# Two chained pair-mixing layers on one core: x before the weights at the start, a full-height bias product, and the first 16 rows of x rebuilt in stage 2 instead of transposed in stage 3

## The chip, the cores and the metric

The kernel runs on one core of a Trainium2 chip. The time is the device time of one execution in microseconds (us). The engines that matter are TensorE (PE, with its weight loads PEld), VectorE (DVE), ScalarE (ACT), GpSimd (POOL) and SyncE (SP), whose work here is to issue DMAs. Each engine executes its own instructions in program order and waits for the others by semaphores. DMAs are issued from SP's, ACT's and POOL's queues.

## What is computed

The input x has 384 x 384 positions (i, j) with 128 channels, all in f32. Two layers follow each other. Of the reference, what matters is this (its names shortened):

```python
z = _layernorm(x, norm_g, norm_b)
left = (z @ Wl + bl) * jax.nn.sigmoid(z @ Wlg + blg)
right = (z @ Wr + br) * jax.nn.sigmoid(z @ Wrg + brg)
core = jnp.einsum('bikh,bjkh->bijh', left, right)
zo = _layernorm(core, onorm_g, onorm_b) @ Wout + bout
g = jax.nn.sigmoid(x @ Wg + bg)
x1 = x + g * zo
...
left = x1 @ W_left + b_left + (x1 @ W_eq + b_eq)
right_sum = jnp.sum(x1 @ W_right + b_right, axis=2, keepdims=True)
out = left * right_sum * jax.nn.sigmoid(x1 @ W_gate + b_gate)
y = _layer_norm(out @ W_out + b_out + x1, ln_scale, ln_bias)
```

The first layer needs a sum over k for every channel h (einsum), so nothing of `core` is complete before all of x has been projected. The second layer works on one row i at a time.

## The kernel before, in words

It runs in three stages. Everything that passes through `seq` keeps its program order on its engine, so the order of the work is the order in which the Python code issues it.

**Opening and stage 1 (lines 99 to 399).** 144 chunks of eight rows and 128 positions k are loaded by SP (`load_chunk`, line 112). The first chunk is loaded in two halves, and SP goes on with the other half and three more chunks, while ACT's queue loads the four projection matrices with two columns of the first norm (`stage`, line 130) and the bias row (line 131). A "step" is four rows. DVE takes mean and variance of each row (`stats`), POOL makes the reciprocal root and the shift (`powers`, `shift`), PE transposes the shifted rows (line 271, in the first step line 288), ACT copies them out of PSUM (`zt`), PE multiplies each with the 128 x 512 matrix `wz` (line 323), ACT applies the sigmoid (line 332), DVE the product (line 334). The shifted transposed rows go to DRAM as `xt_d` (line 294), the shifts as `nd_d` (line 302), the products as `lr_d`.

Before the first such product, `wz` must be made. `busy` (line 147) runs two filler products of 128 x 512 on PE; `fold` (line 154) then makes, for each half of the columns, one product with `m1` (line 163, it needs the weights and two POOL instructions, lines 159 and 160) and one with the bias row `brow`, which has one partition (line 164). `weights` (line 168) adds the two on DVE.

**Stage 2 (lines 443 to 528).** For each channel h, SP loads left and right (`load_h`, lines 93 and 94; called for h+3 in line 506), POOL copies the right part to its own tile (`fill`, lines 468 to 475), PE makes nine products of 128 x 384 (line 493), ACT copies the result (line 502) and squares it, DVE adds to the two sums that the second norm needs, and SP stores to `core_d` (line 509). There are three buffers for loaded channels and two for `rr`. In the last channel DVE and ACT make the reciprocal root of the first 128 rows (lines 419 to 441), which is stored to `rstd_d` (line 525) and loaded back in broadcast (`rt`, line 590).

**Stage 3 (lines 534 to 858).** One turn t of the loop in line 789 does, in this order: `front`, DMA issues, `scale_core(t)`, `layer0(t - 2)`, `gated_left(t - 3)` and, from turn 11 on, `layer1` and the rest of the second layer. `front(f)` runs ahead: it transposes row f of x (three PE transposes into one bank, line 632) if f is below TR = 16, with a copy on ACT or DVE (lines 634 and 636), or takes the row from the tile `xts`, which SP loaded with `nd_d` in broadcast (line 568) and to which POOL's queue added `xt_d` by an accumulating DMA (line 576, from turn 9 on). It also makes the gate of row f - 4 (line 621, sigmoid in line 623). `scale_core` multiplies `core` with the reciprocal root: in the first four rows through a PE broadcast product (`pb`, line 654) and DVE, later with `rt` on POOL (line 657). `layer0` makes `x1T` from it (lines 666 to 669). PSUM is divided in four banks of the pool `ps2` (tag `py`) and four of `ps` (tag `bank`), each used in turn.

Of the kernel before, what the change touches and what calls it, by code (L numbers as in the profile page):

```python
# [8 lines left out]
F32 = mybir.dt.float32  # L9
AF = mybir.ActivationFunctionType  # L10
# [9 lines left out]
def triangle_then_gated_row_kernel(ctx: ExitStack, tc: tile.TileContext, a: dict, out: bass.AP):  # L20
# [10 lines left out]


    nc = tc.nc
    x = a["x"].rearrange("b i j c -> (b i) j c")
# [9 lines left out]
    RG = 4  # L44
    A = 9
    L = 4
    TR = 16
# [6 lines left out]
    xt_d = dpool.tile([C, N, NB, P], F32, name="xt_d")  # L54
    nd_d = dpool.tile([N, N], F32, name="nd_d")

    def seq(ins):

        return tc.keep_in_program_order(ins)
# [4 lines left out]
    def load(dst, src, queue=nc.sync):  # L64
        seq(queue.dma_start(out=dst, in_=src))
# [15 lines left out]
    with ExitStack() as ctx2:  # L81
# [17 lines left out]
        with tc.tile_pool(name="p1w", bufs=6, side="right") as wp, \  # L99
# [28 lines left out]
            wst, g0, b0 = stage[:, 0:4 * H], stage[:, 4 * H:4 * H + 1], stage[:, 4 * H + 1:4 * H + 2]  # L128
            brow, m1, d = stage[0:1, 5 * H:9 * H], stage[:, 9 * H:10 * H], stage[:, 10 * H:10 * H + 1]
            load(stage[:, 0:4 * H + 2], a["L0_side_W"], nc.scalar)  # L130
            load(brow, a["L0_side_b"].rearrange("(o h) -> o h", o=1), nc.scalar)
            load_chunk(0, slice(4, XR))
# [13 lines left out]

            def busy(n):

                for _ in range(n):
                    seq(nc.tensor.matmul(  # L150
                        p0, lhsT=avg, rhs=avg.unsqueeze(1).to_broadcast([P, 4, P]), start=True, stop=True
                    ))

            def fold():

                busy(2)
                seq(nc.gpsimd.tensor_tensor(d, b0, g0, ALU.subtract))
                seq(nc.gpsimd.tensor_tensor(m1, avg, d.to_broadcast([P, P]), ALU.mult))  # L160

                for p, gs in zip((p0, p1), halves):
                    seq(nc.tensor.matmul(p[:, gs], lhsT=m1, rhs=wst[:, gs], start=True, stop=False))
                    seq(nc.tensor.matmul(p[:, gs], lhsT=avg[0:1, :], rhs=brow[:, gs], start=False, stop=True))

# [277 lines left out]
        with tc.tile_pool(name="p2r", bufs=2, side="right", reuse_waits="tile") as rrp, \  # L443
# [14 lines left out]
            def fill(h):  # L458

                if h < H:  # L460
# [15 lines left out]
                    if h == 0:  # L476
                        stay()

            fill(0)
# [54 lines left out]
    with ExitStack() as ctx3:  # L534
# [13 lines left out]

        def work_x(name):

            return lp.tile([P, N], F32, tag="x", name=name)

# [5 lines left out]
        def load_x(i0):  # L558

            if i0 < TR:  # L560
                xt = xin[i0] = xp.tile([P, RG, N], F32, tag="xt", name="xn")
                seq(nc.sync.dma_start(
                    out=xt.rearrange("p i (b c) -> p i b c", b=NB),
                    in_=x[i0:i0 + RG].rearrange("i (b p) c -> p i b c", p=P),
                ))
            elif i0 < N:
                xt = xts[i0] = xp.tile([P, RG, N], F32, tag="xt", name="xt")
                seq(nc.sync.dma_start(
                    out=xt.rearrange("p i j -> p (i j)"),
                    in_=nd_d[i0:i0 + RG].rearrange("i j -> (i j)").partition_broadcast(P),  # L570
                ))
# [8 lines left out]

        def load_core(i0):
            if i0 < N:
                ct = inp.tile([P, RG, N], F32, tag="ct", name="ct")

                for hs in (slice(0, H),) if i0 > 0 else (slice(0, H - 16), slice(H - 16, H)):
                    seq(nc.sync.dma_start(out=ct[hs], in_=core_d[i0:i0 + RG, hs].rearrange("i h j -> h i j")))
                rt = None
# [28 lines left out]
        def front(f):  # L616

            r = rows.get(f - L)
            if r:
                pg = bank("pg")  # L620
                seq(nc.tensor.matmul(pg[:, :N], lhsT=wg0, rhs=r["xT"], start=True, stop=True))  # L621
                gT = r["gT"] = work("gT", fp)
                seq(nc.scalar.activation(gT, pg[:, :N], AF.Sigmoid, bias=bg0))  # L623
            if f < N:
                i0, n = f // RG * RG, f % RG
                if f >= TR:
                    xT = xts[i0][:, n]
                else:
                    xT = work_x("xT")
                    pxt = ps2.tile([P, 512], F32, tag="py", name="pxt") if f < A else bank("pxt")  # L630
                    for s in cols:
                        seq(nc.tensor.transpose(pxt[:, s], xin[i0][:, n, s], ident))
                    if 4 <= f < A:
                        seq(nc.vector.tensor_copy(xT, pxt[:, :N]))
                    else:
                        seq(nc.scalar.copy(xT, pxt[:, :N]))
                rows[f] = {"xT": xT}

# [20 lines left out]
        def layer0(i):  # L659

            r = rows[i]
            m, n = group[i]
            if n == 0:
                quad[m] = {"tot": sp.tile([P, 16], F32, tag="tot", name="tot")}
            pr = bank("pr")
            seq(nc.tensor.matmul(pr[:, :N], lhsT=wc, rhs=r["cs"], start=True, stop=True))  # L666
            seq(nc.vector.scalar_tensor_tensor(pr[:, :N], pr[:, :N], bz, r["gT"], ALU.add, ALU.mult))
            x1T = r["x1T"] = work_x("x1T")
# [223 lines left out]
```

## Time and profile before

| | us |
|---|---|
| three runs, median | 3288.17 |
| lowest and highest | 3287.86, 3288.30 |
| the profiled execution, its own time | 3288.61 |
| its span, from the first to the last record | 3286.8 |

| stretch of the span | us | PE busy | DMA, mean busy share | moved, GB/s |
|---|---|---|---|---|
| 0 to 11.11: until the first product of stage 1 | 11.11 | 9.49 | 0.83 | 213 |
| 11.11 to 1130.80: stage 1 | 1119.69 | 1119.43 | 0.89 | 257 |
| 1130.80 to 1873.90: stage 2 | 743.10 | 743.04 | 0.91 | 282 |
| 1873.90 to 1928.10: first turns of stage 3 | 54.20 | 53.16 | 0.94 | 306 |
| 1928.10 to 3272.90: the rest of stage 3 | 1344.80 | 1341.16 | 0.95 | 265 |
| 3272.90 to 3286.80: after the last product | 13.90 | 0.00 | 0.38 | 108 |

The table is the view of busy time by stretch. "PE busy" counts the modelled ends of the products, which overlap their successors; the time from one product's start to the next is the better measure of what PE gives, and the prediction uses that. An f32 product appears as two records, a transpose as one.

### The profile page before, as it was taken

The numbers are of one execution on the slowest core, as the hardware profiler recorded it, in microseconds if no ns is written. First come the engines' busy times: TensorE is split into PE (matmuls) and PEld (weight loads), VectorE is DVE, ScalarE is ACT, GpSimd is POOL, SyncE is SP. The second block draws the span as 40 slices with busy tenths as digits, with TensorE's granted clock in tenths as the row PEclk, the third lists the DMA queues.
The fourth block names the chain that finished last, engine by engine and source line by source line (L and its number), as shares of the span: only waits on it lengthen the run. The fifth ranks groups of instructions, "written<-read, shape, count | busy, mean of one in ns | idle before, by whom it ended". The sixth has DMA issues, their size and how long they took to land.

```text
span 3286.8 us, 48304 instructions
## 1 busy us (share of the span) xinstructions
PE 3266.3 (99%) x12458; PEld 1987.4 (60%) x12458; DVE 2491.7 (76%) x8019; ACT 1936.1 (59%) x4056; POOL 2289.6 (70%) x3299
## 2 busy tenths in 40 slices
PE   9999999999999999999999999999999999999998
PEld 4444444444444566666666666667777777777776
DVE  7777777777777655555555588888888888888888
ACT  4555555555555533333333467677777777777776
POOL 5555555555555466665656578888888888888997
PEclk9999999999999999999999999999999999999999
DMA  6998998999999499999998999999999999999994
GB/s 165 275 280 257 277 281 258 276 280 264 273 279 269 147 280 287 281 282 286 281 282 284 285 294 264 279 281 270 271 280 275 272 273 280 271 272 273 266 254 127
DMA packets 921492, 873.70 MB, mean 266 GB/s; under 512 B 24657, under 2 KB 836177, under 8 KB 921218
## 3 DMA queue, kind: packets, MB, share of 16 engines
q1 hardware_dynamic: 906528, 796.03, 78.2%
q0 software_dynamic: 13312, 72.55, 12.8%
q8 instruction: 102, 1.67, 0.2%
q10 hardware_dynamic: 1378, 2.04, 0.2%
q14 instruction: 172, 1.41, 0.1%
HBM read 508.63 MB, written 361.89 MB: 265 GB/s over the span
## 4 chain that ended last, share of the span: by engine, by line
PE 96%; POOL 2%; ACT 1%; DVE 1%; issue 1%; DMA 0%; POOLq 0%; ACTq 0%; DVEq 0%
PE pr L323 30%; PE pc L493 22%; PE py L695 7%; PE pr L666 7%; PE pl L684 7%; PE pg L621 7%; PE pg L683 7%; PE pt L271 4%; PE py L696 4%; POOL cs L657 1%; POOL rs L715 1%; POOL yt L765 1%; ACT py L730 0%; DMA core_d<-ct 0%; PE pq L643 0%
## 5 line engine op out<-in xcount | busy, mean ns | idle before, releaser
L323 PE MATMUL pr<-wz,zt 128*128 128x512 f32 x2304 | 1040.0, 593 | 0.0
L332 ACT ACTIVATE sg<-pr,rs 128x256 f32<-128x256 f32 x1152 | 483.8, 471 | 496.6 <-PE pr L323 363.3
L493 PE MATMUL pc<-rr,lrh 128*128 128x384 f32 x2304 | 743.3, 486 | 0.3 <-DVE lr L334 0.3
L334 DVE SCALAR_TENSOR_TENSOR lr<-pr,rs,sg 128x256 f32<-128x256 f32 x1152 | 504.7, 480 | 267.4 <-ACT sg L332 218.2
L323 PEld LDWEIGHTS pr<-wz,zt 128*128 128x128 f32 x2304 | 414.2, 190 | 411.0 <-issue 345.9
L493 PEld LDWEIGHTS pc<-rr,lrh 128*128 128x128 f32 x2304 | 452.0, 196 | 291.8 <-issue 1.1
L730 ACT ACTIVATE py<-py,nm,rs 128x128 f32<-128x128 f32 x1149 | 494.4, 431 | 200.2 <-POOL rs L719 122.1
L657 POOL TENSOR_TENSOR cs<-ct,rt 128x384 f32<-128x384 f32 x380 | 427.9, 1130 | 11.2 <-PE pr L666 6.6
L695 PEld LDWEIGHTS py<-wo,u 128*128 128x128 f32 x2304 | 376.6, 191 | 97.5
L504 DVE TENSOR_TENSOR csum<-csum,ct 128x1152 f32<-128x1152 f32 x127 | 179.3, 1412 | 333.5 <-ACT ct L502 333.5
L765 POOL TENSOR_TENSOR yt<-yt,lnb 128x384 f32<-128x384 f32 x380 | 426.0, 1122 | 3.1 <-DVE yt L759 3.1
L502 ACT COPY ct<-pc 128x1152 f32<-128x1152 f32 x127 | 142.2, 1120 | 445.2 <-PE pc L493 436.0
L695 PE MATMUL py<-wo,u 128*128 128x128 f32 x2304 | 402.1, 275 | 0.0
L252 POOL TENSOR_SCALAR sd<-mv 128x8 f32<-128x8 f32 (+1 forms) x145 | 28.7, 198 | 425.2 <-DVE mv L239 425.0
L262 POOL TENSOR_TENSOR z<-xt,nd 128x512 f32<-128x512 f32 x287 | 299.3, 1043 | 34.6 <-POOL z L262 29.4
L710 DVE BATCH_NORM_STATS2 st<-py 128x6 f32<-128x128 f32 x1152 | 265.5, 286 | 66.9 <-PE py L696 65.1
L696 PE MATMUL py<-ident,x1T 128*128 128x128 f32 x1152 | 314.0, 273 | 0.0
L666 PE MATMUL pr<-cs,wc 128*128 128x384 f32 x768 | 313.9, 490 | 0.1
L684 PE MATMUL pl<-x1T,mat_L_conv_W_left 128*128 128x384 f32 x768 | 311.0, 487 | 1.0 <-ACT gT L623 0.9
L683 PE MATMUL pg<-x1T,mat_L_conv_W_gate 128*128 128x384 f32 x768 | 310.8, 486 | 1.1 <-ACT g L686 0.9
L621 PE MATMUL pg<-xt,mat_L_conv_Wg 128*128 128x384 f32 x736 | 298.6, 487 | 1.4 <-ACT gT L623 1.4
L237 DVE BATCH_NORM_STATS2 st<-xt 128x6 f32<-128x128 f32 x1152 | 273.7, 279 | 3.9 <-DMA xt<-in_x_dram 3.9
(127 smaller groups left out, 4819.0 us busy)
## 6 DMA issues: line engine op xcount, KB each, us to landing
lr_d<-lr SPq DMA_DIRECT2D x128, 1024.0 KB, 7.1
lrh<-lr_d SPq DMA_DIRECT2D x128, 768.0 KB, 7.7
xt_d<-zt SPq DMA_DIRECT2D x288, 256.0 KB, 5.4
xt<-in_x_dram SPq DMA_DIRECT2D x143, 512.0 KB, 6.6
ct<-core_d SPq DMA_DIRECT2D x95, 768.0 KB, 6.1
rt<-rstd_d SPq DMA_DIRECT2D x95, 768.0 KB, 7.7
out_dram<-yt SPq DMA_DIRECT2D x94, 768.0 KB, 8.7
core_d<-ct SPq DMA_DIRECT2D x125, 576.0 KB, 8.8
```

The lines of the kernel that those rows point to most:

```text
L323: seq(nc.tensor.matmul(pr[:, r, :], lhsT=zts[n, q][:, 2 * half + r, :], rhs=wz, start=True, stop=True))
L332: seq(nc.scalar.activation(sg[r], pr[:, r, 2 * H:], AF.Sigmoid, scale=rs[r]))
L334: seq(nc.vector.scalar_tensor_tensor(t[:, :, c * XR + r0 + r, :], pr[:, r, :2 * H].rearrange("k (h s) -> k h s", s=2), rs[r], sg[r].rearra ...
L493: seq(nc.tensor.matmul(banks[ib], lhsT=t[:, kb, ib * P:(ib + 1) * P, 0], rhs=rr[:, kb], start=(kb == 0), stop=(kb == NB - 1),))
L621: seq(nc.tensor.matmul(pg[:, :N], lhsT=wg0, rhs=r["xT"], start=True, stop=True))
L657: seq(nc.gpsimd.tensor_tensor(cs, ct[:, i % RG], rt[:, i % RG], ALU.mult))
L666: seq(nc.tensor.matmul(pr[:, :N], lhsT=wc, rhs=r["cs"], start=True, stop=True))
L683: seq(nc.tensor.matmul(pg2[:, :N], lhsT=wgate, rhs=r["x1T"], start=True, stop=True))
L684: seq(nc.tensor.matmul(pl[:, :N], lhsT=wleft, rhs=r["x1T"], start=True, stop=True))
L695: seq(nc.tensor.matmul(py[:, s], lhsT=r["u"][:, s], rhs=r["wo"], start=True, stop=False))
L730: seq(nc.scalar.activation(py[:, s], py[:, s], AF.Identity, bias=bias, scale=scale))
L765: seq(engine.tensor_tensor(yt, yt, lnbb, ALU.add))
```

## The change

It has three parts.

**At the start**, SP issues the load of the weights itself, second, right after the first half of the first chunk; before, ACT's queue issued it. The bias row gets the full height of 128 partitions: DVE clears `brow`, the bias is loaded in its first partition, and both operands of the bias product have 128 partitions. The filler gets one more product, of 128 x 128.

**In stage 2**, a new function `early_x` puts the first 16 rows of x together: SP loads the row's shifts in broadcast (`xe`, at h = 6 + 5i), POOL's queue adds the row of `xt_d` (h = 8 + 5i), SP stores the sum in a new DRAM tensor `xf_d` (h = 11 + 5i). The tile `xe` uses the three buffers that the reciprocal roots get after stage 2.

**In stage 3**, the first 16 rows come from `xf_d` like the later ones; the transposes and their copies are gone. The gates are made in `front` for the row itself; eight rows are taken ahead before turn 0, with banks of both pools in turn, and the lead shrinks to one row. The orders of the loads of x, of `core_d` and of the roots on SP's queue change; later loads of x are issued some turns later (t + 18 in place of f + 16).

```diff
-    A = 9
-    L = 4
+    A = 8
...
+    xf_d = dpool.tile([C, TR, N], F32, name="xf_d")
...
-            brow, m1, d = stage[0:1, 5 * H:9 * H], stage[:, 9 * H:10 * H], stage[:, 10 * H:10 * H + 1]
-            load(stage[:, 0:4 * H + 2], a["L0_side_W"], nc.scalar)
-            load(brow, a["L0_side_b"].rearrange("(o h) -> o h", o=1), nc.scalar)
+            brow, m1, d = stage[:, 5 * H:9 * H], stage[:, 9 * H:10 * H], stage[:, 10 * H:10 * H + 1]
+            load(stage[:, 0:4 * H + 2], a["L0_side_W"])
...
+            seq(nc.vector.memset(brow, 0.0))
+            load(brow[0:1], a["L0_side_b"].rearrange("(o h) -> o h", o=1), nc.scalar)
...
                 busy(2)
+                busy(1, 1)
...
-                    seq(nc.tensor.matmul(p[:, gs], lhsT=avg[0:1, :], rhs=brow[:, gs], start=False, stop=True))
+                    seq(nc.tensor.matmul(p[:, gs], lhsT=avg, rhs=brow[:, gs], start=False, stop=True))
...
+            def early_x(h):
+                for n, step in enumerate((6, 8, 11)):
+                    i, odd = divmod(h - step, 5)
+                    if not odd and 0 <= i < TR:
+                        if n == 0:
+                            early[i] = rp.tile([P, N], F32, tag="ve", name="xe", bufs=NB)
+                            seq(nc.sync.dma_start(out=early[i], in_=nd_d[i].partition_broadcast(P)))
+                        elif n == 1:
+                            seq(nc.gpsimd.dma_start(
+                                out=early[i], in_=xt_d[:, i].rearrange("c b k -> c (b k)"), accum_op=ALU.add
+                            ))
+                        else:
+                            seq(nc.sync.dma_start(out=xf_d[:, i], in_=early.pop(i)))
...
             for h in range(H):
                 fill(h + 1)
+                early_x(h)
...
-        xp, lp, fp, inp = pool("p3x", 6), pool("p3l", 20), pool("p3f", A), pool("p3in", 3)
+        xp, lp, fp, inp = pool("p3x", 6), pool("p3l", 19), pool("p3f", A + 3), pool("p3in", 3)
...
+                    in_=xf_d[:, i0:i0 + RG].rearrange("c i j -> c (i j)") if i0 < TR
+                    else nd_d[i0:i0 + RG].rearrange("i j -> (i j)").partition_broadcast(P),
...
         def front(f):
+            r = rows[f] = {"xT": xts[f // RG * RG][:, f % RG]}
+            pg = ps2.tile([P, 512], F32, tag="py", name="pg") if f < A and f % 2 == 0 else bank("pg")
+            seq(nc.tensor.matmul(pg[:, :N], lhsT=wg0, rhs=r["xT"], start=True, stop=True))
+            gT = r["gT"] = work("gT", fp)
+            seq(nc.scalar.activation(gT, pg[:, :N], AF.Sigmoid, bias=bg0))
...
-        for i0 in range(0, 3 * RG, RG):
-            load_x(i0)
-        load_core(0)
-        load_x(3 * RG)
-        load_core(RG)
+        load_x(0)
+        load_x(RG)
+        load_core(0, between=lambda: load_x(2 * RG))
+        load_core(RG)
+        load_x(3 * RG)
...
-            while f < min(N + L, t + max(L, A - t // 3)):
+            while f < min(N, t + max(1, A - t // 2)):
...
-            if t >= 2 and fetched <= f + 16:
+            if t >= 2 and fetched <= t + 18:
```

`between` is called in `load_core(0)` after the load of the first 112 channels of `core_d`, so the third load of x stands between the two parts of the first load of `core_d`.

More of the change, by code (lines that the diff above doesn't have):

```diff
@@ L145, in triangle_then_gated_row_kernel, with busy @@
             p0, p1 = (pps.tile([P, 2, 4 * H], F32, tag="pr", name=n)[:, 0] for n in ("p0", "p1"))
-            def busy(n):
+            def busy(n, cols=4):
                 for _ in range(n):
                     seq(nc.tensor.matmul(
-                        p0, lhsT=avg, rhs=avg.unsqueeze(1).to_broadcast([P, 4, P]), start=True, stop=True
+                        p0[:, :cols * P], lhsT=avg, rhs=avg.unsqueeze(1).to_broadcast([P, cols, P]),
+                        start=True, stop=True,
                     ))
@@ L477, in fill @@
                         stay()
+            def early_x(h):
[11 more added lines that the diff above has]
+                            seq(nc.sync.dma_start(out=xf_d[:, i], in_=early.pop(i)))
+            early = {}
             fill(0)
@@ L547, in work @@
             return pool.tile([P, N], F32, tag=name, name=name)
-        def work_x(name):
-            return lp.tile([P, N], F32, tag="x", name=name)
         cols = [slice(b * P, (b + 1) * P) for b in range(NB)]
@@ L558, in load_x @@
         def load_x(i0):
[L560 to L566, printed above, removed]
+            if i0 < N:
                 xt = xts[i0] = xp.tile([P, RG, N], F32, tag="xt", name="xt")
@@ L569, in load_x @@
                     out=xt.rearrange("p i j -> p (i j)"),
-                    in_=nd_d[i0:i0 + RG].rearrange("i j -> (i j)").partition_broadcast(P),
+                    in_=xf_d[:, i0:i0 + RG].rearrange("c i j -> c (i j)") if i0 < TR
+                    else nd_d[i0:i0 + RG].rearrange("i j -> (i j)").partition_broadcast(P),
                 ))
@@ L579, in add_x, with load_core @@
                 ))
-        def load_core(i0):
+        def load_core(i0, between=None):
             if i0 < N:
@@ L586, in load_core @@
                     seq(nc.sync.dma_start(out=ct[hs], in_=core_d[i0:i0 + RG, hs].rearrange("i h j -> h i j")))
+                    if between and hs.start == 0:
+                        between()
                 rt = None
@@ L616, in front @@
         def front(f):
[L618 to L637, printed above, removed]
+            r = rows[f] = {"xT": xts[f // RG * RG][:, f % RG]}
[3 more added lines that the diff above has]
+            seq(nc.scalar.activation(gT, pg[:, :N], AF.Sigmoid, bias=bg0))
         def right_sums(i0, i1):
@@ L667, in layer0 @@
             seq(nc.vector.scalar_tensor_tensor(pr[:, :N], pr[:, :N], bz, r["gT"], ALU.add, ALU.mult))
-            x1T = r["x1T"] = work_x("x1T")
+            x1T = r["x1T"] = work("x1T", lp)
             seq(nc.vector.scalar_tensor_tensor(
```

## The prediction

> **What bounds the kernel now.** I read the page first: busy shares and the chain that ended last.
>
> ```profile
> PE 3266.3 (99%) x12458; PEld 1987.4 (60%) x12458; DVE 2491.7 (76%) x8019; ACT 1936.1 (59%) x4056; POOL 2289.6 (70%) x3299
> ...
> PE 96%; POOL 2%; ACT 1%; DVE 1%; issue 1%; DMA 0%; POOLq 0%; ACTq 0%; DVEq 0%
> ```
>
> TensorE is the bound in every stage, so only PE work taken away, or a wait of PE taken away, counts. All of it must come from three places: the opening, the crossing from stage 2 to 3, and stage 2 as a possible loser. So I went on to PE's timeline at both places. First the opening, weight loads (start, duration, line), then what DVE and POOL waited for:
>
> ```profile
> 5.36 0.50 PEld L163 LDWEIGHTS p<-stage 128*128 128x128 f32 x2 [2.11 <-POOL stage L160]
> 6.51 0.50 PEld L164 LDWEIGHTS p<-stage,avg 1*128 1x128 f32 x2 [0.65 <-issue]
> 9.96 0.71 PEld L288 LDWEIGHTS pt<-ident,z 128*128 128x128 f32 x4 [0.65 <-POOL sd L252]
> 12.13 0.33 PEld L323 LDWEIGHTS pr<-wz,zt 128*128 128x128 f32 x1 [0.52 <-issue]
> 12.98 0.33 PEld L323 LDWEIGHTS pr<-wz,zt 128*128 128x128 f32 x1 [0.52 <-issue]
> 13.62 0.19 PEld L323 LDWEIGHTS pr<-wz,zt 128*128 128x128 f32 x1 [0.30 <-issue]
> 14.05 0.19 PEld L323 LDWEIGHTS pr<-wz,zt 128*128 128x128 f32 x1 [0.24 <-issue]
> ...
> 4.63 0.19 POOL L159 TENSOR_TENSOR stage<-stage 128x1 f32<-128x1 f32 x1 [3.33 <-DMA stage<-in_L_side_W_dram]
> 4.95 0.49 DVE L237 BATCH_NORM_STATS2 st<-xt 128x6 f32<-128x128 f32 x2 [3.93 <-DMA xt<-in_x_dram]
> ```
>
> A pass of 512 columns takes 0.85 us (12.13 to 12.98) and from 13.62 on 0.43: PE runs at half clock until about 13.4. Weights land at 4.6, x at 4.95.
>
> The crossing, PE's products (two records per f32 product, three per transposed row):
>
> ```profile
> 1873.98 0.49 PE L632 MATMUL pxt<-ident,xn 128*128 128x128 f32 x3
> 1875.03 1.20 PE L632 MATMUL pxt<-ident,xn 128*128 128x128 f32 x9 [0.56 <-ACT ct L517]
> 1876.28 0.91 PE L621 MATMUL pg<-xT,mat_L_conv_Wg 128*128 128x384 f32 x2
> 1877.03 0.49 PE L632 MATMUL pxt<-ident,xn 128*128 128x128 f32 x3
> 1877.36 0.81 PE L621 MATMUL pg<-xT,mat_L_conv_Wg 128*128 128x384 f32 x2
> ...
> 1880.71 0.88 PE L621 MATMUL pg<-xT,mat_L_conv_Wg 128*128 128x384 f32 x2 [0.26 <-DVE xT L634]
> ...
> 1881.76 0.81 PE L654 MATMUL pb<-r,ident 128*128 128x384 f32 x2
> ```
>
> From start to start a transposed row costs 0.33 (1877.03 to 1877.36) and a 384-column product 0.645 (1888.66 to 1889.31 and on). Last, stage 2 in one step:
>
> ```profile
> 1404.01 0.36 SPq L93 DMA_DIRECT2D lrh<-lr_d  x1
> 1406.24 0.99 POOL L474 COPY rr<-lrh 128x768 f32<-128x768 f32 x1 [1.56 <-DMA lrh<-lr_d]
> 1407.17 1.54 POOL L475 COPY rr<-lrh 128x256 f32<-128x256 f32 x1
> 1409.78 1.12 ACT L502 COPY ct<-pc 128x1152 f32<-128x1152 f32 x1 [3.49 <-PE pc L493]
> ```
>
> PE's step ends about 1409.6; the copies that the next needs end at 1408.71, so a loaded channel arrives with some 0.9 us to spare.
>
> **Stage 3, what goes.** Of 16 rows 16 x 0.33 = 5.3 us of PE leave, with the 11 ACT copies (0.47 each) and 5 DVE copies (0.50) beside them. Waits leave too. I count PE from 1873.98 to the product `pr` of row 4 (line 666) at 1895.13: 21.15 us. In it are 23 products of 0.645 (9 gates, 4 `pb`, 4 `pr`, 6 of `gated_left`), 14.84, and 13 transposed rows, 4.29. So 2.0 us were waits: bank, first copies, DVE copy, first `x1T`.
>
> **Stage 3, what comes.** After: until the same product PE has 25 products (11 gates), 16.1 us, and no transpose. Waits, one by one: gate 1 wants a bank of the last channel, free when ACT's copy of line 517 ends (1874.98): 1875.03 instead of 1874.63, 0.40. Gates 1 to 7 end at 1879.55. The first `pb` wants the root; its DVE chain ends at 1880.10 now and nothing moves it: 0.65. The first `cs` on DVE wants the last 16 channels of `core_d`, issued at 1877.65 when their store has landed, 4.9 us to landing, so 1882.55; `cs` 0.56 makes `pr` of row 0 ready about 1883.2 against 1882.75: 0 to 0.45. Row 4 wants `rt`, issued at 1886.65 after the root's store, POOL at 1890.9 and 1.0 long: 1891.9 against 1891.6: 0 to 0.35. Together 1.05 to 1.85, I take 1.45. Gain: (5.3 + 2.0) - 1.45 = 5.85 us, bounds 5.4 and 6.25. ACT has its table (1.28, from 1875.75) and 8 sigmoids of 0.51 done by 1881.2; each bank is free before its product comes. The tail does not change: after 3272.9 PE is idle in both.
>
> SP's queue there: the four loads of x are as large as before, in longer rows. The fourth now stands behind `rt`, which keeps SP until 1886.65; it was issued at 1878.01. It lands about 1894 (7 us, the shortest that these loads took), and gate 12 comes about 1897. Behind it `ct`, `rt` and the loads of rows 16 and 20 shift by 768 KB, about 2.4 us at the 329 GB/s of 1905 to 1925: row 16 at about 1899.5 where POOL waited for them until 1897.60. POOL's accumulating DMA then holds `cs` of row 9 until about 1901.4; its `pr` comes about 1904. Cost 0, with 3 us of cover. Later x loads come at t + 18 where buffers are free already; now SP waits 347 us in all there for DVE. I take that at nothing: rows are wanted 18 turns later. Its bound is +-1 us, since PE lost only 3.6 us in the rest of stage 3.
>
> **Stage 2, what comes.** Per row: two issues on SP of 0.36, ahead of line 93, where SP waits 4.2 us per step (438 by 104) for PE; one on POOL of 0.82 to 0.93 (lines 525, 576), after line 475, where POOL is idle 0.9 and then 1.5 us before the next landing. Both hidden. The bytes are not free: a row is 0.197 MB three times. From stage 2's row (91.2% of 600 us for 169.3 MB) a plain one costs 0.635 us of all 16 engines; from stage 3 an accumulating one (32.3% of 500 us for 31.46 MB) 1.01: 2.28 us per five steps, where 8.5% of 29 us = 2.46 are free. It just fits. The Trainium skill (DMA: Bandwidth & Descriptors, "Issuing engines are not separate DMA queues") says that DMAs of all issuing engines share the same 16 DMA engines and interleave, so POOL's queue adds no room. By the row there is room for all but nothing over; by the rule with the page's HBM limit of about 358 GB/s (an estimate) the fullest step, 1.63 MB (169.3 by 104 steps) and the 0.39 of two plain ones, takes 5.7 of its 5.80 us. A late load has 0.9 us before PE stands. I take 0.25 us for 16 rows; bounds 0 (no gain is possible, since PE waits for nothing there) and, were nothing of it free, 16 x 2.28 = 36.
>
> **The opening.** Weights are issued at 1.22 in place of 0.73 and queue behind x: POOL starts about 5.1, the fold about 5.85 (+0.5). x no longer shares with them: about 0.4 earlier, 4.55; the chain of DVE and POOL then gives `z` at about 9.05 in place of 9.46. The added filler (about 0.45) fills what PE would wait. The DVE clearing, nearest row the memset of `avg` (0.17), four times as wide, lies before x lands. The bias product costs the same: with one partition it took 1.15 us, as the full one did. By itself the opening would lose 0.5.
>
> What the height may do is the clock. The skill (TensorE: Matmul & The Clock Gate, "What's actually happening") says that full clock comes after one busy window of some 3.4 us, windows running freely. By that rule the window before the one that ended at 13.4 (6.6 to 10.0) should have done: line 163 and 164 filled it back to back. By the rows it did not; half of it were products of one partition, and their activity seems not to have counted. I go with the row: full height makes that window count, clock at 10.0. Then the fold ends at 10.2 (3.6 of 4 products at 1.15, the rest at half), first product at about 11.15 as now, and its six passes take 2.6 in place of 3.63: gain 1.0. If height is nothing to the clock: fold until 10.45, first product at 11.75, 1.9 slow passes, loss 0.25. If even the window to 6.6 counts, 2.3 gained, held by `z`. DVE, with six steps of statistics ahead of its first product, ends them about 15.5 and frees the bank at 16.4; PE wants it at 17.1.
>
> **Sum** against the profiled 3288.61 (span 3286.8 and 1.81 around it): 5.85 + 1.0 - 0.25 = 6.6, so 3282.0; the median lies 0.44 lower: **3281.6**.
>
> **Rivals.** (1) Height changes no clock: 5.85 - 0.25 - 0.25 = 5.35: 3282.8. For it: the gaps of 0.65 between the fold's loads may be what made the window idle; they stay. 27%. (2) Clock already at 6.6: 7.9: 3280.3. 12%. (3) New queueing at the crossing: the fourth x load and what lies behind it arrive over 3 us later than I put them, PE stands for 2 to 3: 3283.6 to 3284.6. For it: DMA engines are at 0.94 there; against: long rows. 8%. (4) Slower: stage 2's DMA engines are full. The nine-tenths share becomes a bound, loads slip past the 0.9 us and PE waits in the steps of the 16 rows. It decides from (6.6 + 0.25)/16 = 0.43 us lost per row; if half of the 2.28 does not fit, 18 us lost: 3300. Against: stage 3 runs at 0.95 and PE hardly waits. 5%. The forecast itself: 48%.
>
> **Numbers.** 0.2%, about what a measurement of this kernel can tell from no change, is 6.6 us: 3281.6 is the very bound. Half of the main case and rival 2 are beyond it: faster 0.40; same 0.55; slower 0.05. The range, 3280.0 to 3284.4, leaves out rival 4 and the ends of 2 and 3.
>
> **What would show it.** Passes of 0.43 from the first product of stage 1 (clock); PE's wait before the first `pb` about 0.65; no transposes between 1870 and 1905; PE without waits in stage 2, line 474 later by under 1 us in the steps of the 16 rows; POOL not late with row 9. I am wrong if passes stay at 0.85 until 13.4, if gate 12 waits for a DMA, or if stage 2 grows.

## The result, and the profile after

The kernel after takes 3282.53 us (median of 17 runs, 3281.12 to 3283.23), the kernel before in the same comparison 3288.28 (17 runs, 3286.81 to 3289.53): ratio 0.9982, 95% interval 0.9976 to 0.9988, 5.75 us less. The profiled execution took 3282.93, its span is 3281.2 in place of 3286.8.

TensorE is still the bound. First the page of the kernel after: busy time by engine, and the shares of the chain that ended last.

```profile
PE 3257.7 (99%) x12412; PEld 1982.5 (60%) x12412; DVE 2488.3 (76%) x8015; ACT 1929.3 (59%) x4045; POOL 2286.7 (70%) x3315
...
PE 95%; POOL 3%; DVE 1%; ACT 1%; issue 0%; DMA 0%; POOLq 0%; DVEq 0%; ACTq 0%
```

There are 46 PE instructions fewer: 48 transposes and one filler more, which counts twice. Next, busy time by stretch of the kernel after (stretch, its length, then busy time and instructions of PE, PEld, DVE, ACT and POOL, granted clock, DMA share, GB/s). The cuts stand at the same events as in the table of before.

```profile
0.00:8.81 8.81, 7.64 (x18) 4.42 (x19) 4.27 (x23) 1.86 (x3) 4.43 (x16) 1.00 0.79 221
8.81:1128.00 1119.19, 1118.51 (x3480) 551.18 (x3481) 853.48 (x3448) 621.58 (x1457) 615.85 (x866) 1.00 0.89 257
1128.00:1871.10 743.10, 743.08 (x2304) 452.16 (x2305) 404.14 (x258) 292.03 (x258) 454.63 (x780) 1.00 0.95 295
```

The opening is 2.30 shorter (8.81 for 11.11), stage 1 0.5 shorter, stage 2 as long as before to a hundredth, at a DMA share of 0.95 for 0.91. (In the first microseconds the clock column says 1.00 because the clock's record begins with its first change; there the pitch of the passes tells the clock.)

The rest I read from the starts of single products. "T0" is the start of the first PE instruction after stage 2's last product:

| | before | after | difference |
|---|---|---|---|
| first product of stage 1 | 11.11 | 8.81 | -2.30 |
| from there to T0 | 1862.87 | 1862.33 | -0.54 |
| T0 to the start of the last PE instruction | 1398.62 | 1394.91 | -3.71 |
| from there to the span's end | 14.24 | 15.11 | +0.87 |
| sum | 3286.84 | 3281.16 | -5.68 |

The two remarkable rows are the third, where 5.85 was forecast, and the last, which the prediction had at nothing. First the opening of the kernel after: PE's weight loads, then the first work of DVE on x and of POOL on the weights:

```profile
4.62 0.34 PEld L153 LDWEIGHTS p<-avg 128*128 128x128 f32 x1 [0.52 <-issue]
5.12 0.50 PEld L168 LDWEIGHTS p<-stage 128*128 128x128 f32 x2 [0.16 <-POOL stage L165]
5.71 0.76 PEld L169 LDWEIGHTS p<-stage,avg 128*128 128x128 f32 x2
6.56 0.63 PEld L168 LDWEIGHTS p<-stage 128*128 128x128 f32 x2
7.22 0.41 PEld L169 LDWEIGHTS p<-stage,avg 128*128 128x128 f32 x2
7.76 0.25 PEld L293 LDWEIGHTS pt<-ident,z 128*128 128x128 f32 x2
8.33 0.20 PEld L293 LDWEIGHTS pt<-ident,z 128*128 128x128 f32 x2 [0.33 <-POOL z L288]
8.78 0.30 PEld L328 LDWEIGHTS pr<-wz,zt 128*128 128x128 f32 x2 [0.25 <-ACT zt L294]
...
3.64 0.49 DVE L242 BATCH_NORM_STATS2 st<-xt 128x6 f32<-128x128 f32 x2 [2.08 <-DMA xt<-in_x_dram]
4.40 0.19 POOL L164 TENSOR_TENSOR stage<-stage 128x1 f32<-128x1 f32 x1 [3.10 <-DMA stage<-in_L_side_W_dram]
```

The fold starts at 5.12 (5.36 before) and from 6.56 on the weights of its products come at about half the former pitch: 0.66 and 0.54 apart, where before they came 1.15 apart. The trace's own record of the clock grants full speed at 7.00 here and at 13.39 in the kernel before.

The crossing of the kernel after, PE's products and ACT's copies of the last channel:

```profile
1871.14 0.81 PE L638 MATMUL pg<-xt,mat_L_conv_Wg 128*128 128x384 f32 x2
1873.68 4.78 PE L638 MATMUL pg<-xt,mat_L_conv_Wg 128*128 128x384 f32 x14 [1.73 <-ACT ct L540]
1879.62 0.88 PE L657 MATMUL pb<-r,ident 128*128 128x384 f32 x2 [1.16 <-DVE r L446]
```

```profile
1869.16 0.20 ACT L514 ACTIVATE warm<-mhalf 128x1 f32<-128x1 f32 x1
1871.47 0.48 ACT L534 COPY ct<-pc 128x384 f32<-128x384 f32 x1 [2.11 <-DMA core_d<-ct]
...
1872.83 0.80 ACT L540 COPY ct<-pc 128x768 f32<-128x768 f32 x1 [0.32 <-issue]
```

The first copy of channel 127 (line 534) comes 0.33 after T0, where the kernel before had it 1.87 ahead of T0. It waited 2.11 us for a buffer `ct`: there are two, and the store of channel 125 from one of them, issued by ACT at 1860.89, took 10.5 us to land (6.9 in the kernel before). Gate 1 waits for the second copy, the root for the sums behind the first one. So one late store moves everything here by about 2 us.

### The profile page after: what moved, and what is told of

Same layout as the page of the kernel before. It is cut to its first block, busy times and chain, and to the rows that moved or that the text cites. A ratio compares the mean times of both kernels' runs of the same rounds, so it can differ in the third digit from the quotient of the medians.

```text
span 3281.2 us, 48289 instructions
## 1 busy us (share of the span) xinstructions
PE 3257.7 (99%) x12412; PEld 1982.5 (60%) x12412; DVE 2488.3 (76%) x8015; ACT 1929.3 (59%) x4045; POOL 2286.7 (70%) x3315
## 3 DMA queue, kind: packets, MB, share of 16 engines
q8 instruction: 102, 1.67, 0.2%
## 4 chain that ended last, share of the span: by engine, by line
PE 95%; POOL 3%; DVE 1%; ACT 1%; issue 0%; DMA 0%; POOLq 0%; DVEq 0%; ACTq 0%
PE pr L328 30%; PE pc L516 22%; PE py L698 7%; PE pr L669 7%; PE pl L687 7%; PE pg L686 7%; PE pg L638 7%; PE pt L276 4%; PE py L699 4%; POOL cs L660 1%; POOL rs L718 1%; POOL yt L768 1%; ACT py L733 0%; DMA core_d<-ct 0%; DVE st L713 0%
## 5 line engine op out<-in xcount | busy, mean ns | idle before, releaser
L638 PE MATMUL pg<-xt,mat_L_conv_Wg 128*128 128x384 f32 x768 | 310.7, 487 | 3.3 <-ACT ct L540 1.7
L479 POOL COPY rr<-lrh 128x768 f32<-128x768 f32 x128 | 177.0, 1383 | 152.2 <-DMA lrh<-lr_d 151.9
```

## The experiments

Theory 1: the opening gains because the full clock comes earlier (1a by the height of the bias product, 1b by the filler and the earlier weights). Theory 2: the crossing falls short because the new loads of x hold back that store. Theory 3: the early rows cost stage 2 nothing. Theory 4 came up on the way: something of the early rows lengthens the end of the program. Times are medians beside the kernel before in the same comparison, whose median lay between 3288.28 and 3289.09. Where an interval reaches 1.0, the time alone shows no difference, and what is said there rests on the profile.

| kernel | time | against before | ratio, 95% interval |
|---|---|---|---|
| after | 3282.53 | -5.75 | 0.9982, 0.9976 to 0.9988 |
| opening_alone | 3285.19 | -3.13 | 0.9991, 0.9984 to 0.9997 |
| one_row_bias | 3282.85 | -5.47 | 0.9984, 0.9977 to 0.9992 |
| height_alone | 3286.30 | -2.02 | 0.9994, 0.9985 to 1.0002 |
| weights_on_act | 3283.84 | -4.48 | 0.9985, 0.9979 to 0.9992 |
| store125_sp | 3281.71 | -7.13 | 0.9978, 0.9970 to 0.9986 |
| short_rows | 3281.99 | -6.85 | 0.9981, 0.9973 to 0.9989 |
| early_alone | 3290.06 | +1.22 | 1.0004, 0.9996 to 1.0012 |
| early_more | 3282.78 | -6.06 | 0.9982, 0.9975 to 0.9988 |
| early_no_pool | 3288.57 | -0.11 | 0.9999, 0.9990 to 1.0007 |
| early_no_store | 3289.57 | +0.89 | 1.0002, 0.9993 to 1.0010 |
| four_ahead | 3286.45 | -2.23 | 0.9991, 0.9983 to 1.0000 |
| dve_add_sp_store | 3279.94 | -9.15 | 0.9973, 0.9962 to 0.9983 |

### The opening

**opening_alone** has the first part of the diff and nothing of the other two.

> The kernel before with the first part of the change alone (x first, weights second on SP's queue, bias product of full height, short filler); stages 2 and 3 as before. Theory 1 (the two traces: full clock at 7.0 us in place of 13.4, first product of stage 1 at 8.8 in place of 11.1, and 0.55 less in stage 1): about -2.9 us, 3285.4, first product at 8.8. Rival (the prediction's step, clock only one window earlier): -1.0, 3287.3, first product at 11.1. Rival (the earlier start belongs to the whole change's different memory layout, not to these lines): 0 to -0.5.

Measured: -3.13, first product at 8.79, full clock at 6.90. The gain of the opening belongs to these lines.

**one_row_bias**: the kernel after with

```diff
-            brow, m1, d = stage[:, 5 * H:9 * H], stage[:, 9 * H:10 * H], stage[:, 10 * H:10 * H + 1]
+            brow, m1, d = stage[0:1, 5 * H:9 * H], stage[:, 9 * H:10 * H], stage[:, 10 * H:10 * H + 1]
...
-            seq(nc.vector.memset(brow, 0.0))
...
-                    seq(nc.tensor.matmul(p[:, gs], lhsT=avg, rhs=brow[:, gs], start=False, stop=True))
+                    seq(nc.tensor.matmul(p[:, gs], lhsT=avg[0:1, :], rhs=brow[:, gs], start=False, stop=True))
```

> The kernel after, with the bias product back to one partition on both operands (and no clearing of the row); load order and filler as after. Theory 1a (the height makes the window count): the full clock comes one or two windows later, 10.4 or 13.8 us, first product of stage 1 at 10.0 to 11.2, time 1.2 to 2.9 above after, 3283.7 to 3285.4. Theory 1b (it is the filler and the earlier weights, which leave no gap before the fold; the first window is already filled by the two fillers before any bias product runs): clock at 7.0, first product 8.8, 3282.5 as after.

Measured: clock at 5.68 and first product at 8.79 in the profiled run, median 0.3 above the kernel after. So the height wasn't necessary for it in this execution: 1a in this form falls. But the 16 runs spread from 3281.96 to 3286.73, those of the kernel after from 3281.12 to 3283.23.

**height_alone**: the kernel before with the height alone.

```diff
-            brow, m1, d = stage[0:1, 5 * H:9 * H], stage[:, 9 * H:10 * H], stage[:, 10 * H:10 * H + 1]
+            brow, m1, d = stage[:, 5 * H:9 * H], stage[:, 9 * H:10 * H], stage[:, 10 * H:10 * H + 1]
...
-            load(brow, a["L0_side_b"].rearrange("(o h) -> o h", o=1), nc.scalar)
...
+            seq(nc.vector.memset(brow, 0.0))
+            load(brow[0:1], a["L0_side_b"].rearrange("(o h) -> o h", o=1), nc.scalar)
...
-                    seq(nc.tensor.matmul(p[:, gs], lhsT=avg[0:1, :], rhs=brow[:, gs], start=False, stop=True))
+                    seq(nc.tensor.matmul(p[:, gs], lhsT=avg, rhs=brow[:, gs], start=False, stop=True))
```

> The kernel before with the bias product of full height alone (row cleared by DVE, bias loaded after that); weights stay on ACT's queue and no short filler. Theory 1a (height): full clock at 10.0 or 6.6 us, first product of stage 1 no earlier than x allows (z at 9.46), 10 to 10.5, -0.7 to -2: 3286.3 to 3287.6. Theory 1b (gap before the fold decides, not height): full clock at 13.4 as before, first product 11.1, 3288.3.

Measured: clock at 7.10, first product at 9.79, -2.02. So the height is sufficient, and 1b alone falls too: in these executions either did it. (The interval reaches 1.0002, but the 13 runs lie between 3286.22 and 3287.35.) The changes of the clock in these traces lie multiples of 3.41 us apart, so I read the windows of that length that end at a change (or, in the kernel before, the one before it). Busy time by stretch, one row each of the kernel before, height_alone, early_alone (below, it has the opening of the kernel before) and weights_on_act (below):

```profile
6.56:9.98 3.42, 3.42 (x8) 1.47 (x7) 1.36 (x8) 0.00 (x0) 2.97 (x7) 1.00 1.21 291
```

```profile
3.69:7.10 3.41, 2.93 (x6) 1.51 (x5) 1.88 (x12) 0.00 (x0) 1.33 (x4) 1.00 1.18 310
```

```profile
4.38:7.79 3.41, 2.59 (x9) 1.18 (x8) 2.71 (x17) 0.00 (x0) 1.82 (x4) 1.00 1.20 301
```

```profile
6.25:9.66 3.41, 2.06 (x11) 1.29 (x9) 3.33 (x20) 0.14 (x1) 2.82 (x7) 1.00 1.21 290
```

The second column is PE's busy time. The kernel before was busy for all of 6.56 to 9.98 and got no full clock at its end; height_alone with 2.93 did. early_alone had been granted full speed at 4.38 and lost it again at 7.79, after 2.59 busy; weights_on_act kept it with 2.06. What sets the first and the third apart is that half of their fold is products of one partition. By the starts of its products, early_alone's window held 1.55 us of full height and 1.04 of one partition; at the crossing below, a window with 1.51 busy lost the clock and one with 1.68 kept it. So such a product fills PE's record but hardly counts for the clock. The kernel after has PE busy with full products from 1.05 to 8.3, so that a full window ends by 7.9 however the windows lie; with one partition it depends on how they lie. That the spread of one_row_bias comes from this is not shown: most of its runs were only timed.

How much the place of the windows matters, the other profiles show. Three more have the opening of the kernel before (early_alone, early_no_pool and early_no_store, all below): they had full clock by 3.87 to 5.18, lost it again by 10.69 at the latest, and got it back at 14.11 to 15.42; their first product came at 9.84 to 10.23. All nine with the full height had it by 7.27 and kept it through the opening. T0 lay at 1873.29 to 1874.47 in the four with the old opening and at 1871.05 to 1871.30 in the seven with the whole new one. So opening and stage 1 together gain 2.0 to 3.4, and the 2.84 of the two profiles is one draw.

**weights_on_act**: the kernel after with the weights on ACT's queue.

```diff
-            load(stage[:, 0:4 * H + 2], a["L0_side_W"])
+            load(stage[:, 0:4 * H + 2], a["L0_side_W"], nc.scalar)
```

> The kernel after, with the load of the weights back on ACT's queue; bias product of full height and short filler stay. Theory 2 (x that lands 1.3 us earlier is what sets the first product once the clock is up): x's statistics start at 4.9 in place of 3.6, first product at 9.9 in place of 8.8, time +1.0: 3283.5. If the clock alone sets it and x has room: first product 8.8, 3282.5. If the weights then land later and a gap opens before the fold, the clock also falls back by a window (10.4) and the first product comes at 10 or later, +1.5 to +2.3.

Measured: clock at 6.25, but x's statistics at 5.05 in place of 3.64, first product at 9.94, and a distance to before 1.27 smaller. Once the clock is up, x sets the first product: height_alone, whose x also lands late (4.90), stops at 9.79. So of the 2.3 us, some 1.3 come from the clock alone (11.11 to 9.79) and the last 1.0 need x first (9.79 to 8.81).

### The crossing

**store125_sp**: the kernel after with

```diff
-                    queue = nc.sync if h < H - 3 else nc.scalar
+                    queue = nc.sync if h < H - 2 else nc.scalar
```

> The kernel after, with the store of channel 125 moved from ACT's queue to SP's, ahead of the loads of x (the stores of 126 and 127 stay on ACT's). Theory 2 (the shortfall of the crossing is that store, held back by the x loads that SP issues beside it; ACT's first copy of channel 127 waits 2.11 us for its buffer, and behind it the bank of gate 1, the root and the first product with the root): that wait is gone, gate 1 starts about 1 us after the last product of stage 2 in place of 2.54, the first product with the root 1.6 to 2.1 us earlier, time 1.5 to 2 lower: 3280.5 to 3281.0. Rival (the later loads of core_d and of the root set the order anyway): the copy comes earlier but the first product of row 0 does not, 3282.3 to 3282.6.

ACT's first copy and PE's products of store125_sp:

```profile
1869.22 0.20 ACT L514 ACTIVATE warm<-mhalf 128x1 f32<-128x1 f32 x1
1869.33 0.46 ACT L534 COPY ct<-pc 128x384 f32<-128x384 f32 x1
```

```profile
1871.20 0.81 PE L638 MATMUL pg<-xt,mat_L_conv_Wg 128*128 128x384 f32 x2
1872.25 4.78 PE L638 MATMUL pg<-xt,mat_L_conv_Wg 128*128 128x384 f32 x14 [0.24 <-ACT ct L540]
1877.46 0.88 PE L657 MATMUL pb<-r,ident 128*128 128x384 f32 x2 [0.43 <-DVE r L446]
...
1889.00 0.91 PE L669 MATMUL pr<-cs,wc 128*128 128x384 f32 x2 [0.34 <-POOL cs L660]
```

The copy's wait is gone, the first product of row 0 comes 2.15 earlier than in the kernel after. Row 4's wait for the root's load takes 0.5 of that back; at row 15 it is 1.55, and small differences in the remaining 1340 us leave 0.9 in this profile. The distance to before grows by 1.4, a little less than the 1.5 to 2 expected. Theory 2 holds, its rival has the 0.5.

**short_rows**: `xf_d` is kept as `[C, TR, NB, 2 * P]`, of which the first 128 of each 256 are used, so stage 3 loads x in pieces of 512 bytes.

> The kernel after, with the 16 rows kept in DRAM in pieces of 512 bytes with gaps, so that their loads in stage 3 (and their stores in stage 2) move 512 bytes at a time in place of 6144 (1536); bytes, queues and order are the same. Theory 2a (it is the length of the rows that lets SP's loads crowd out the store of channel 125 on ACT's queue): ACT's wait for that store falls from 2.11 to under 0.5, as in the kernel before; the x loads take longer (SP held some 2.5 us for each issue, as before), time 0.5 to 2 lower. Theory 2b (the bytes in flight do it, whatever the row): the wait stays at 1.5 to 2.5, time 3282.5 or above, since shorter pieces also land later and gate 0 may wait.

Measured: ACT's copy starts right behind its predecessor, without a wait, as 2a says; the store of channel 125 took 7.3 us to land (10.5 after, 6.9 before). The load of `core_d`, which SP issues 7.2 us ahead of T0 in the kernel after (3.0 before), is not enough to hold the store back: in short_rows it comes 6.9 ahead. But the third load of x now lands late. PE's products in short_rows:

```profile
1877.55 0.88 PE L663 MATMUL pb<-r,ident 128*128 128x384 f32 x2 [0.42 <-DVE r L446]
1880.10 1.62 PE L644 MATMUL pg<-xt,mat_L_conv_Wg 128*128 128x384 f32 x2 [1.67 <-DMA xt<-xf_d]
1881.52 2.36 PE L663 MATMUL pb<-r,ident 128*128 128x384 f32 x4
```

Gate 8 waits 1.67 for x, and the two products that took 0.81 now take 1.62: the clock had fallen at 1879.91. This profiled run (3285.02) is the slowest of the 14; the fastest is 3281.43. So the length of the rows decides whether the store is crowded out (one profile each; in the kernels after and like it the wait varied, 0.66 to 2.54), but shorter rows are no clean cure: by the medians they gain 1.1 of the 1.4 that store125_sp gains, with a wider spread. The Trainium skill (DMA: Bandwidth & Descriptors, "Queues, rings and completion order") says that each DMA engine takes turns among its queues a whole packet at a time; 10.5 for 7.3 us would fit that, though no run here shows the packets of one engine in order.

**four_ahead**: the kernel after with four gates ahead.

```diff
-    A = 8
+    A = 4
```

> The kernel after with four gates taken ahead before the first turn in place of eight. Theory 5 (the gates ahead are what PE does while the root is made; the root's end does not move): gates 4 to 7, 4 products of 0.645, no longer stand before the first product with the root, whose wait grows from 1.16 by 2.6; PE is the bound later, so the 2.6 stay: 3285.1. Rival (later waits of this stretch shrink by the same, since rows 4 and on wait for their loads anyway): 3282.5 to 3283.5.

Measured: the distance to before falls from 5.75 to 2.23, more than the 2.6, and the profiled run (3288.83, near the top of a spread from 3283.68 to 3289.26) is 5.9 above that of the kernel after. Its wait for gate 1, and its stretches:

```profile
1874.03 2.93 PE L638 MATMUL pg<-xt,mat_L_conv_Wg 128*128 128x384 f32 x6 [2.17 <-ACT ct L540]
...
1871.94:1875.36 3.42, 1.33 (x4) 0.87 (x5) 2.50 (x5) 2.11 (x4) 0.00 (x0) 1.00 0.81 227
1875.36:1878.77 3.41, 1.60 (x3) 0.34 (x1) 3.22 (x3) 3.37 (x6) 0.00 (x0) 0.50 0.80 248
1875.36:1885.60 10.24, 7.33 (x12) 3.50 (x11) 5.54 (x7) 3.95 (x7) 5.47 (x4) 0.50 0.75 236
1885.60:1890.00 4.40, 4.40 (x15) 2.57 (x14) 3.74 (x9) 1.16 (x2) 2.08 (x3) 1.00 0.95 325
```

Theory 5 has its 2.6 (4 products of 0.645), the root is 0.3 later, and on top PE runs at half clock from the first product with the root (1879.87) to 1885.60, 5.7 us of which half, 2.9, are lost: 5.8 in all, as from T0 to the last product. The fall itself is not the missing gates' doing: its window ends at 1875.36, and with gate 1 at 1874.03 and 0.645 for each, gate 4 could not have started before 1875.97. It is the wait of 2.17 us (1.73 in the kernel after). But the gates would have brought the clock back sooner: in the next window PE was busy for 1.60, and four more products at half clock, 5.2 us (an estimate from their 0.645), would have filled it; in short_rows a window with 3.22 busy was enough. How often the clock falls in the runs that were only timed is not known.

### Stage 2 and the end of the program

**early_alone** has the early rows in the kernel before, where nothing reads them.

> The kernel before, with the rows of x put together in stage 2 as in the change, but not used: stage 3 still transposes x. So it does work that nothing reads. Theory 3 (the transfers of the 16 rows fit beside stage 2): stage 2 keeps its 743.1 us, time 3288.0 to 3288.6, within 0.3 of before. Rival (the DMA engines are full): 0.43 us or more for each row, 7 us or more, 3295 and above.

Measured: stage 2 took 743.12, so Theory 3 holds, and yet the time is 1.22 above before. 0.87 lies behind the last product (15.11 for 14.24).

**early_more**: the kernel after with three more stores of each early row.

> The kernel after, with three more stores of every early row (to tensors that nothing reads): per row 0.59 MB more. By the prediction's sum (2.28 us of all 16 DMA engines for a row, 2.46 free in five channels, 0.635 for each further plain transfer) 4.19 are wanted and 1.73 are missing: 28 us lost over 16 rows, 3310. Rival (the busy share counts waiting in the engines and overstates the use, there is more room): PE loses under 0.2 us for a row, 3282.5 to 3285.

Stage 2's busy time in early_more, then in the kernel before:

```profile
1150.00:1600.00 450.00, 450.00 (x1397) 273.77 (x1396) 234.42 (x156) 177.27 (x156) 267.59 (x482) 1.00 0.99 320
```

```profile
1150.00:1600.00 450.00, 450.00 (x1397) 273.82 (x1396) 246.82 (x156) 176.72 (x155) 282.17 (x464) 1.00 0.91 283
```

At a DMA share of 0.99 and 320 GB/s PE still waits for nothing in stage 2 (743.12). The rival's time holds: the prediction's free room of 2.46 us in five channels was far too small. That the busy share counts waiting, the rival's reason, is not shown. ACT's first copy of channel 127 waited 0.66 here, 1.45 less than in the kernel after, and row 16 came 1.44 earlier after T0: the crossing follows this wait.

**early_no_pool** and **early_no_store** are early_alone without one of the three steps:

```diff
-                        elif n == 1:
-                            seq(nc.gpsimd.dma_start(
-                                out=early[i], in_=xt_d[:, i].rearrange("c b k -> c (b k)"), accum_op=ALU.add
-                            ))
```

```diff
-                        else:
-                            seq(nc.sync.dma_start(out=xf_d[:, i], in_=early.pop(i)))
```

> The kernel before with the unused early rows, but without POOL's accumulating step: SP loads the shifts and stores them, nothing more (so the new tensor holds only shifts, and nothing reads it). In all five runs with early rows the time from the last product to the end of the span was 15.06 to 15.16 us, in the four without them 14.2 to 14.3. Theory 4a (POOL's 16 DMAs of stage 2 lengthen the end of the program): 14.2 here, time as before, 3288 to 3289. Theory 4b (the 32 DMAs of SP, or the new tensor): 15.1 here, time 0.8 above before.

> The kernel before with the unused early rows, but without the store of the sum (nothing of them leaves the chip's memory). Theory 4a (POOL's 16 DMAs lengthen the end): 15.1 us from the last product to the end, time 0.8 above before. Theory 4b (SP's DMAs or the new tensor, which is not written here): 14.2, or between if each of SP's DMAs counts.

What SP's queue waited for in the last microseconds (total, times, longest), first in early_no_pool, then in early_no_store:

```profile
SPq L903 <- PEq L903: 3.3, 2, 2.4
SPq L903 <- DMA out_dram<-yt: 1.7, 1, 1.7
```

```profile
SPq L905 <- PEq L905: 4.1, 2, 3.7
SPq L905 <- DMA out_dram<-yt: 1.7, 1, 1.7
```

Line 903 or 905 is the `with` around the whole kernel, whose end is the closing exchange of semaphores. Without POOL's 16 DMAs of stage 2 SP waits 3.3 there for PE's queue and the end takes 14.22; with them, and without a store of the early rows, 4.1 and 15.11. The times point the same way (-0.11 and +0.89), but both intervals hold 1.0. What carries it are the profiles: 14.22 to 14.24 in the five without these DMAs, 15.11 or more in the nine with them. So Theory 4a: the cost hangs on POOL's DMAs. Why one answer in the closing exchange takes 3.7 us in place of 2.4 because of DMAs that ended some 1600 us before, no run here shows.

**dve_add_sp_store** puts two findings together: the kernel of store125_sp, and

```diff
-                for n, step in enumerate((6, 8, 11)):
+                for n, step in enumerate((6, 9, 11)):
...
+                            row[i] = rp.tile([P, N], F32, tag="r", name="xr", bufs=NB)
                             seq(nc.sync.dma_start(out=early[i], in_=nd_d[i].partition_broadcast(P)))
+                            seq(nc.sync.dma_start(out=row[i], in_=xt_d[:, i].rearrange("c b k -> c (b k)")))
                         elif n == 1:
-                            seq(nc.gpsimd.dma_start(
-                                out=early[i], in_=xt_d[:, i].rearrange("c b k -> c (b k)"), accum_op=ALU.add
-                            ))
+                            seq(nc.vector.tensor_add(early[i], early[i], row.pop(i)))
```

> The kernel after, with two of the findings put together: the store of channel 125 on SP's queue, and the 16 early rows added by DVE (SP loads the row of x beside its shifts, DVE adds the two) in place of POOL's accumulating DMAs. Theory 2 and theory 4a together: no wait of ACT for the store of 125 (gate 1 about 1 us after the last product of stage 2, the first product with the root about 6.3 after it), 14.2 us from the last product to the end in place of 15.1, stage 2 at 743.1 as before since DVE has 45 % of it free; time 1.3 and 0.85 below after, some 8 below the kernel before: 3280.2 to 3280.7 where before is 3288.3 to 3288.8. Rival (DVE's 16 additions delay the sums of stage 2, or the end of the program lengthens for another reason): 3281.5 or above, or stage 2 longer than 743.5.

Measured: 3279.94, 9.15 below before, the largest gain of all. PE's products at the crossing and SP's waits at the end:

```profile
1872.32 4.78 PE L638 MATMUL pg<-xt,mat_L_conv_Wg 128*128 128x384 f32 x14 [0.24 <-ACT ct L540]
1877.53 0.88 PE L657 MATMUL pb<-r,ident 128*128 128x384 f32 x2 [0.42 <-DVE r L446]
```

```profile
SPq L891 <- PEq L891: 3.3, 2, 2.4
...
SPq L891 <- DMA out_dram<-yt: 1.7, 1, 1.7
```

T0 to the last product is 1393.41 (1394.91 after), the end 14.23 (15.11), stage 2 743.1. In the profiled executions it is 2.25 faster than the kernel after (3280.68 for 3282.93), as expected; the medians lie further apart (2.6, and 3.4 by the distances to before), of which the 1.2 beyond is not explained.

## Why the prediction was right, and where two errors met

The forecast of 3281.6 was 0.9 below the time, and the time lies in its range. But its sum 5.85 + 1.0 - 0.25 was in fact 3.71 + 2.84 + 0 - 0.87: two terms were off by 2.1 and 1.8, in opposite directions, and a third was missing. The parts of the change were named rightly; that the total came so close is luck.

**The opening, 1.0 forecast, 2.84 measured.** The step that failed is "I go with the row: full height makes that window count, clock at 10.0". The direction was right (height_alone shows that height brings the clock), but the clock came at 7.0, a whole window earlier, which was rival 2 with its 12%. Three things were missed. The prediction took the window ends of one trace for fixed; with the full height the first full clock lay between 4.02 and 7.27, another time in each profile. The added filler does not only "fill what PE would wait": with it the window that ends at 7.0 is full (height_alone shows that a window need not be). And the weights, forecast 0.5 later behind x, landed 0.23 earlier (POOL at 4.40 for 4.63), x itself 1.3 earlier (3.64 for 4.95) and not 0.4. So `z` did not hold the first product: its two instructions end at 8.28, not at 9.05. The 0.54 in stage 1 are the cold passes less a wait of PE for POOL's shift in the third step, 0.59. The first six passes take 2.65 in place of 3.79, so 1.14; the prediction had 2.6 and 3.63.

**Stage 3, 5.85 forecast, 3.71 measured.** The listed waits were right in kind and, in store125_sp, nearly in size: gate 1 starts 1.05 after T0, of which 0.645 is gate 0, so 0.40 (forecast 0.40); the first product with the root waits 0.69 (0.65); row 0 loses 0.07 (0 to 0.45); row 4 waits 0.5 (0 to 0.35). From T0 to the first product of row 4 store125_sp takes 17.80 us where the prediction's terms give 16.1 + 1.45 = 17.55. The kernel after takes 19.52. The step that failed is "the root; its DVE chain ends at 1880.10 now and nothing moves it": ACT's first copy waits for the store of channel 125, and 2.1 us of root and bank go with it. The prediction looked for new queueing at the fourth load of x (rival 3, 8%); that one was not waited for, and gate 12 came at 1897.10, where it was forecast. The first two loads did the harm, to a store on another queue. This is not all of the 2.1 missing: without the wait store125_sp is 1.6 ahead of the kernel after at row 16, 0.9 at the last product and 1.4 by the medians. The rest stays open, and two profiles can't settle it: the six with stage 3 as before took 1397.75 to 1400.08 from T0 to the last product.

**Stage 2, 0.25 forecast, 0 measured.** Right, and for a better reason than was given: it did not "just fit". early_more put another 1.9 us of transfers on a row and lost nothing, so rival 4 was further away than 5% said. (By its own 91.2% the free share is 8.8%, not 8.5%, and its 5.7 us are 5.65; neither changes the term.)

**The end, 0 forecast, +0.87 measured.** "The tail does not change" was true of the engines' work (DVE's last instruction ends 7.9 after the last product in both) and false of the closing exchange.

**Later loads of x, 0 to within 1 us.** Right as far as the profiles go: PE's waits in the rest of stage 3 are 3.2 us before and 3.3 after.

## What to carry to other kernels

When a chain decides a crossing, list every buffer that its first instruction writes, and ask when the transfer that frees it lands beside the transfers that the change starts earlier. Keep the tensor engine's first products gap-free and of full height, and put the first operand of the longest chain first in the queue. A cost that shows in no stage may stand in the program's closing: compare the time from the last product to the end, too.

## What was not expected of the hardware

- **The clock falls without an idle window.** In four_ahead PE was busy for 1.33 of the 3.42 us before the fall, in short_rows for 1.51 of 3.41 (1876.50 to 1879.91); in the kernel after 1.68 of 3.41 (1870.68 to 1874.09) were enough to keep it. The Trainium skill (TensorE: Matmul & The Clock Gate, "What's actually happening") gives one idle window of about 3.4 us as the condition for the fall; here waits of 2.17 and 1.67 us did it. The measurement decides: at such a crossing a wait can have a second price, 3.41 us at half clock in short_rows and 10.24 in four_ahead. The windows of the kernel after and of short_rows:

```profile
1870.68:1874.09 3.41, 1.68 (x5) 0.69 (x5) 2.08 (x4) 1.80 (x3) 0.00 (x0) 1.00 0.97 291
```

```profile
1876.50:1879.91 3.41, 1.51 (x4) 0.31 (x3) 0.87 (x2) 1.74 (x4) 2.19 (x3) 1.00 1.00 275
```

- **A product of one partition does not count like a full one** for the clock, though it takes the same 1.15 us.
- **The DMA engines' busy share is no measure of what is left**: 0.91 and 283 GB/s became 0.99 and 320 without a wait of PE in stage 2.
- **POOL's 16 accumulating DMAs in stage 2 made the program's end 0.9 us longer** (15.11 for 14.22 us).
